# Adding two half tiles by DMA in two transfers of 64 partitions, with the adjacency copied by ScalarE, in a four-layer graph kernel

## The chip, the cores and the metric

The kernel runs on one core of a Trainium2 chip. Time is device time of one execution in microseconds (us); lower is better. The core has four compute engines, each with its own queue of instructions that it takes in order: PE (matmul), DVE (VectorE), ACT (ScalarE) and POOL (GpSimd). A fifth queue, SP, only issues transfers. Transfers are carried by 16 DMA engines that all queues share. SBUF is the working memory of 128 partitions; PSUM, in eight banks of 128 x 512 floats, takes what PE writes.

## The reference, cut to what matters

Four layers, each a residual on a normalised and rectified input. `x` is (64, 256, 128), `adj` (256, 256), all float32.

```python
h = jnp.maximum(_layernorm(x, axis=-1), 0.0); x = x + _L0_gnn_ref(h, adj, adj, ..., 5)   # gated, 5 steps
h = jnp.maximum(_layernorm(x, axis=-1), 0.0); x = x + _L1_gnn_ref(h, adj, adj, Theta1, bias)
h = jnp.maximum(_layernorm(x, axis=-1), 0.0); x = x + _L2_gnn_ref(h, adj, weight, bias)
h = jnp.maximum(_layernorm(x, axis=-1), 0.0); x = x + _L3_gnn_ref(h, adj, b_lin, a, adj)

def _L3_gnn_ref(x, W, b_lin, a, bias):
    ...
    pre = s1[:, :, None, :] + s2[:, None, :, :] + b_lin
    h = jnp.where(pre >= 0, pre, ALPHA * pre)
    e = jnp.einsum('bije,e->bij', h, a) + bias
    attn = jax.nn.softmax(e, axis=2)
    out = jax.nn.sigmoid(jnp.einsum('bij,bjf->bif', attn, x))
    return out
```

The last layer is most of the work: for each of 64 batches and each of 256 x 256 pairs of nodes, 256 features are passed through a leaky rectifier and summed with the weights `a`.

## The kernel before

**Slots and tiles.** The batches are taken in 32 pairs. The scores `e` of a pair are made in 64 slots; a slot stands for four rows `i` in each of two batches. The 256 features lie on the 128 partitions in two halves. So a slot has two tiles, half 0 and half 1, each of 128 partitions x 2048 floats (1 MB), from a ring of 14 (line 99). A tile holds, for every pair of nodes, the smaller (or the rectified difference) of a row of `s1` and all of `s2`. PE then sums over the partitions with a window of signs (`win`, `win_n`) into a bank of scores (`score`, lines 1025 to 1049, matmul on line 1041): four groups of 32 columns for a tile, which stand in the profile as eight matmul records.

**Who makes a tile.** `work_on_tile` (line 933): half 0 is made by DVE in one instruction (line 953), half 1 by ACT in eight (line 961), and POOL makes either in eight (line 967), whichever is behind.

**Added slots.** In a share of the slots, `SHARE` = 4/13 (lines 25 and 893, 600 of the 1952 slots that are not among the last 96), half 1 is made by POOL in the sign of half 0, and the two tiles are added by a DMA that POOL issues: `add_pair` (lines 985 to 993) takes the tile `z` and adds it to `t` in place (`accum_op=OP.add`, line 987). The sum is scored once, where an unjoined slot is scored twice.

**The bank of scores.** A unit is 32 slots, that is, half of the nodes `i` of a pair of batches. Its bank is filled before its first scoring, by `fill_bank` (lines 1004 to 1007): DVE writes `adj_n` (the bias of the scores) plus `lin`, a row that is the same for all `i` and comes to all partitions by a broadcast DMA (`rows`, line 783). When a unit is scored in full, `tail` (lines 827 to 882) makes softmax and output from the bank: two instructions on line 839, maximum, exponential, transpose, product, tanh, and the store. Units of the first pair (`alone`) are filled by PE instead and get their `lin` in the tail (line 834).

**Fronts.** The first three layers, and the projections that the fourth needs, are `front` (lines 498 to 821), one for each pair of batches, run beside the slots of an earlier pair. They use all four engines.

**The order.** It is fixed when the kernel is built. A planner (lines 1096 to 1137) keeps a clock for each engine, takes the engine that is earliest, and gives it what is ready by its own estimates: `ran(engine, us, ...)` adds an estimated duration. The estimates are constants: `PROJECT`, `TURN` and others on lines 471 to 473, and `ISSUE, ADDED, LANDED = 0.65, 5.3, 6.6` on line 29 for an added pair (POOL's issue, the spacing of two additions, the time from issue to landing). The order of each engine is then kept as program order; where an estimate is too short, an engine waits at run time with all behind it.

Of the kernel before, what the change touches and what calls it, by code (L numbers as in the profile page):

```python
# [10 lines left out]
OP = mybir.AluOpType  # L11
# [3 lines left out]
P = 128  # L15
NB = 2
# [5 lines left out]
MOST_POSITIVE = -MOST_NEGATIVE  # L22
PE, DVE, ACT, POOL = ENGINES = (mybir.EngineType.PE, mybir.EngineType.DVE, mybir.EngineType.Activation, mybir.EngineType.Pool)
SLOTS = 64
SHARE = (4, 13)
AHEAD_OF = 2
ALONE = 96
LOW = 1
# [4 lines left out]
def kernel(  # L33
# [50 lines left out]
    nc = tc.nc  # L84
    B, N, D = x.shape
# [20 lines left out]
    def ran(engine, us, *after):  # L106
        start = max(clock[engine], 0.0, *after)
        clock[engine] = start + us
        return clock[engine] + SEEN[engine]
# [10 lines left out]
    def of_spare(bank):  # L120

        return [b for b in spare if bank < 2 or id(b[0]) in WRITTEN]
# [14 lines left out]
    def by_feature(b, nb=NB):  # L137
        return b[:, 0:nb * N].rearrange("p (b n) -> p b n", b=nb)
# [329 lines left out]
    SHORT = dict(tag="short", bufs=12)  # L468


    PROJECT, MIX, TURN, PRODUCT, PRODUCTS = (None, 0.44, 0.86), (None, 0.88, 1.74), (None, 0.38, 0.60), (None, 0.45, 0.88), (None, 1.33, 2.64)
    COPY, BIASED, TANH, ELEMENTS = (None, 0.32, 0.48), (None, 0.40, 0.58), (None, 0.40, 0.57), (None, 0.36, 0.61)
    NORMED, STATS, LAST = (None, 0.78, 1.55), (None, 0.50, 0.87), (None, 0.55, 1.04)

    def norm(src, since, h):

        nb = src.shape[1]
        stats = work.tile([P, nb * NC, 3], F32, name="stats", bufs=4)
        mv = work.tile([P, nb * NC, 2], F32, name="mv", bufs=4)
        s, h = rows_of(src), rows_of(h)[:, :, 0:D]  # L480
        yield DVE, since
        for k in range(0, nb * NC, 2):
            nc.vector.bn_stats(stats[:, k:k + 2, :].rearrange("p k s -> p (k s)"), s[:, k:k + 2, :].rearrange("p k d -> p d k"))
        nc.vector.tensor_reduce(mv[:, :, 0], stats[:, :, 1:2], AX.X, OP.add, negate=True)
        t = ran(DVE, STATS[nb], since) + 0.1
        yield POOL, t
        inverse_root(mv[:, :, 1], stats[:, :, 2], 1.0 / D, OP.mult, LN_EPS, OP.add)
        nc.gpsimd.tensor_mul(mv[:, :, 0], mv[:, :, 0], mv[:, :, 1])  # L488
        t = ran(POOL, 1.69, t)
        yield ACT, t  # L490
        for k in range(nb * NC):
            nc.scalar.activation(h[:, k, :], s[:, k, :], AF.Relu, bias=mv[:, k, 0:1], scale=mv[:, k, 1:2])  # L492
        return ran(ACT, NORMED[nb], t)

    READY = {}
# [331 lines left out]
    def tail(u, pe, since):  # L827

        ops = READY[u]
        x3, h3, pe = ops["x3"], ops["h3"], [by_feature(pe[0])[:, k, :] for k in range(NB)]  # L830
        yield DVE, max(since, ops["t_lin"])
        used = banks_of.pop(u)[0]
        if ops["alone"]:
            nc.vector.tensor_add(by_feature(used), by_feature(used), ops["lin"].to_broadcast([P, NB, N]))
            since = ran(DVE, ELEMENTS[2], since, ops["t_lin"])
            yield DVE, since
        sc = feat("sc", **SHORT)
        for k, (b, c) in enumerate(across(u)):
            nc.vector.scalar_tensor_tensor(sc[:, k, :], ops["s2o"][:, b, :], ops["s1o"][:, b, c:c + 1], pe[k], op0=OP.min, op1=OP.add)
        t = ran(DVE, 0.8, since)  # L840
        spare.append([used, t])
        yield DVE, t
        nmx = work.tile([P, NB], F32, name="nmx")
        nc.vector.tensor_reduce(nmx, sc, AX.X, OP.max, negate=True)
        t = ran(DVE, ELEMENTS[2], t)
        yield ACT, t
        for b in range(NB):
            nc.scalar.activation(sc[:, b, :], sc[:, b, :], AF.Exp, bias=nmx[:, b:b + 1], scale=1.0)
        t_s = ran(ACT, 0.8, t)
        yield PE, t_s, 1  # L850
        b = take()
        to_token(b[0], sc)
        t = ran(PE, TURN[2], t_s, b[1])
        yield ACT, t
        wT = tok("wT", **SHORT)
        nc.scalar.copy(wT, by_token(b[0]))
        t = ran(ACT, COPY[2], t)
        spare.append([b[0], t])
        yield PE, t, 1
        bank = take()  # L860
        po = bank[0][:, :NB * (D + 1)].rearrange("p (b d) -> p b d", b=NB)
        for k, (b, _) in enumerate(across(u)):
            for c in range(NC):
                side_by_side(po[:, k, :], wT[:, k, c, :], h3[:, b, c, :], c == 0, c == NC - 1)
        t = ran(PE, PRODUCT[2], t, bank[1])
        yield DVE, t
        rs = work.tile([P, NB], F32, name="rs")
        nc.vector.reciprocal(rs, po[:, :, D])
        t = t_s = ran(DVE, 0.15, t)
        yield ACT, t  # L870
        for k in range(NB):
            nc.scalar.activation(po[:, k, 0:D], po[:, k, 0:D], AF.Tanh, scale=rs[:, k:k + 1])
        t = ran(ACT, 0.9, t, t_s)
        yield DVE, t
        o = work.tile([P, NB, D], F32, name="o")
        nc.vector.scalar_tensor_tensor(o, po[:, :, 0:D], 0.5, x3[:, 0] if ops["alone"] else x3[:, :, u[1], :], op0=OP.mult, op1=OP.add)
        t = ran(DVE, 0.36, t)
        spare.append([bank[0], t])
        p, k = u
        nc.sync.dma_start(out[p * NB + k].rearrange("(c p) d -> p c d", p=P) if ops["alone"] else  # L880
                          out[p * NB:(p + 1) * NB, k * P:(k + 1) * P, :].rearrange("b p d -> p b d"), o)
        TAILED.add(u)
# [101 lines left out]

    def add_pair(n):
        (since, t, e), (since_z, z, e_z) = pairs[n][0], pairs.pop(n)[2]
        nc.gpsimd.dma_start(out=t.rearrange("p g b n -> p (g b n)"), in_=z.rearrange("p g b n -> p (g b n)"), accum_op=OP.add)  # L987
        issued = ran(POOL, ISSUE, since, since_z)
        done = adding[0] = max(adding[0] + ADDED, issued + LANDED)
        held[e] -= 1  # L990
        held[e_z] -= 1
        tiles.append([z, done])
        made.append((done, n, 2, t, None))
# [3 lines left out]
    def bank_ready():  # L997

        u = next((u for u in UNITS if u not in left and u not in banks_of), None)
        if u not in READY or READY[u]["alone"] or len(banks_of) == 2 or all(where(slot(k))[0] < u for k in range(3)):  # L1000
            return None
        return (max(READY[u]["t_lin"], min(b[1] for b in of_spare(2))), u) if of_spare(2) else None

    def fill_bank(u):
        bank, free = take(2)
        nc.vector.tensor_add(by_feature(bank), adj_n[:, u[1]:u[1] + 1, :].to_broadcast([P, NB, N]), READY[u]["lin"])  # L1006
        banks_of[u] = bank, ran(DVE, ELEMENTS[2], free, READY[u]["t_lin"])

    def score_ready():

# [85 lines left out]
    while scored[0] < 2 * NSLOT or CHAINS:  # L1096
        while begun_fronts[0] < NPAIR and begun_fronts[0] < 2 + (scored[0] + 2 * SLOTS - 1) // (2 * SLOTS):
            begin_front()
        e = min(now, key=now.get)
        todo = []  # L1100
        for key in CHAINS:
            since = chain_ready(key, e)
            if since is not None:
                todo.append((since, (0, key) if isinstance(key, tuple) else (1, key), key))
        if e == PE:
            best = score_ready()
            if best:
                todo.append((best[0], (2,), best[1]))
        else:
            since = tile_ready(e)  # L1110
            if since is not None:
                todo.append((since, (3,), None))
            if e == DVE and bank_ready():
                todo.append((bank_ready()[0], (2,), bank_ready()[1]))
            pair = pair_ready()
            if e == POOL and pair and e not in begun:
                todo.append((pair[0] + SLACK, (2,), pair[1]))
        ready = [x for x in todo if x[0] <= now[e] + 0.05]
        if ready:
            if e == PE and len(tiles) <= LOW:  # L1120
                ready = [x for x in ready if x[1] == (2,)] or ready
            _, (rank, *_), what = min(ready, key=lambda x: x[1])
            if rank < 2:
                advance(what)
            elif e == PE:
                score(what)
            elif e == DVE and rank == 2:
                fill_bank(what)
            elif rank == 2:
                add_pair(what)  # L1130
            else:
                work_on_tile(e)
            in_order()
            now[e] = max(now[e], clock[e])
        else:
            later = [x[0] for x in todo] + [t for t in now.values() if t > now[e]]
            now[e] = min(later) if later else now[e] + 1.0
# [31 lines left out]
```

## Time and profile before

| | us |
|---|---|
| median of 2 runs | 4814.04 (4812.59 to 4815.49) |
| the profiled execution | 4794.9 |
| its span, first to last instruction | 4793.1 |

The granted clock of PE was 0.997 over the span. The lines below are for orientation; those that the argument needs are shown with it. A line of the costliest groups names the source line, engine and operation, output and inputs, shapes and count; behind the bar stand the busy time in us, the mean duration of one in ns, and the idle time just before them with what ended it. Durations of one include its start-up, so that instructions in a row overlap and the busy time is less than count times mean.

```profile
L1041 PE MATMUL bank<-rl,win_n 128*32 128x512 f32 x17864 | 2226.3, 594 | 19.9 <-DMA rl<-rl 13.4
L1041 PE MATMUL bank<-rl,win 128*32 128x512 f32 x10104 | 1349.9, 594 | 0.0
L987 POOL DMA_DIRECT2D rl<-rl x600 | 651.7, 1105 | 9.4 <-issue 4.8
rl<-rl POOLq DMA_DIRECT2D x600, 1024.0 KB, 8.1
```

The first two are the scorings, 27968 records for 3496 of them. The third are the 600 additions as POOL issues them; the fourth, from the list of DMA issues, has their size and the median time from issue to landing.

### The profile page before, as it was taken

To read this page: it belongs to the slowest core of one execution; us is meant where nothing else is said; L and a number is where in the kernel's file an instruction comes from. 1 tells how busy PE (TensorE), PEld (TensorE's weight loads), DVE (VectorE), ACT (ScalarE), POOL (GpSimd) and SP (SyncE) were. 2 spreads that over 40 slices of the span, in tenths; PEclk is the share of its full clock that TensorE was granted. 3 is DMA by queue.
4 is the path that set the end of the run, shared out by engine and by line. 5 is a ranking of instruction groups with operands and counts; after the bars stand their busy time and mean duration, and the time that the engine had idled before them with its cause. 6 is when DMAs were issued, how large, how long until landed. Compare 5 with 4: busy or idle time off the path is not lost.

```text
span 4793.1 us, 132928 instructions
## 1 busy us (share of the span) xinstructions
PE 4718.4 (98%) x51591; PEld 1740.7 (36%) x51591; DVE 4647.5 (97%) x3502; ACT 4659.3 (97%) x12220; POOL 4619.2 (96%) x9823
## 2 busy tenths in 40 slices
PE   9999999999999999999999999999999999999999
PEld 4333333333333333333333333333333333333333
DVE  5999999999999999999999999999999999999998
ACT  5999999999999999999999999999999999999999
POOL 2999999999999999999999999999999999999998
PEclk9999999999999999999999999999999999999999
DMA  0777777777777777777777777777767776777730
GB/s 23 157 143 152 146 152 150 144 149 154 152 143 154 146 146 157 147 151 145 150 146 155 149 148 147 149 151 154 148 139 153 155 150 142 145 151 148 147 69 5
DMA packets 131523, 672.70 MB, mean 140 GB/s; under 512 B 14920, under 2 KB 50120, under 8 KB 54088
## 3 DMA queue, kind: packets, MB, share of 16 engines
q0 software_dynamic: 86400, 629.18, 65.5%
q1 hardware_dynamic: 43768, 35.01, 2.5%
q8 instruction: 403, 6.60, 0.5%
q14 instruction: 232, 1.90, 0.1%
q10 hardware_dynamic: 720, 0.00, 0.0%
HBM read 26.48 MB, written 8.52 MB: 7 GB/s over the span
## 4 chain that ended last, share of the span: by engine, by line
PE 47%; DVE 15%; POOL 11%; ACT 8%; DMA 4%; issue 4%; POOLq 0%; DVEq 0%; ACTq 0%
PE bank L1041 31%; PE bank L414 14%; DVE rl L953 11%; POOL rl L967 9%; ACT rl L961 6%; DMA rl<-rl 4%; PE bank L447 1%; POOL rl L987 1%; DVE bank L1006 1%; ACT h L492 1%; PE bank L439 0%; DVE bank L626 0%; POOL mv L409 0%; DVE hT L630 0%; DVE d L622 0%
## 5 line engine op out<-in xcount | busy, mean ns | idle before, releaser
L961 ACT ACTIVATE rl<-bank,s1b 128x256 f32<-128x256 f32 x10104 | 4072.5, 833 | 10.1 <-DMA rl<-rl 6.5
L953 DVE TENSOR_TENSOR rl<-s1a,bank 128x2048 f32<-128x2048 f32 x1743 | 3894.9, 2277 | 26.1 <-DMA rl<-rl 13.1
L967 POOL TENSOR_SCALAR rl<-s2n,s1b 128x256 f32<-128x256 f32 x6280 | 3033.4, 829 | 13.9 <-DMA rl<-rl 3.1
L1041 PE MATMUL bank<-rl,win_n 128*32 128x512 f32 x17864 | 2226.3, 594 | 19.9 <-DMA rl<-rl 13.4
L1041 PE MATMUL bank<-rl,win 128*32 128x512 f32 x10104 | 1349.9, 594 | 0.0
L967 POOL TENSOR_SCALAR rl<-s2c,s1a 128x256 f32<-128x256 f32 x2440 | 1190.6, 783 | 5.2 <-PE bank L1041 1.4
L1041 PEld LDWEIGHTS bank<-rl,win_n 128*32 128x32 f32 x17864 | 583.5, 110 | 1181.0 <-issue 964.9
L987 POOL DMA_DIRECT2D rl<-rl x600 | 651.7, 1105 | 9.4 <-issue 4.8
L1041 PEld LDWEIGHTS bank<-rl,win 128*32 128x32 f32 x10104 | 335.1, 110 | 675.6 <-issue 529.4
L414 PE MATMUL bank<-mT,wts 128*32 128x512 f32 x2480 | 325.6, 595 | 4.5 <-DVE rh L587 4.5
L414 PE MATMUL bank<-adj_t,h 128*32 128x256 f32 x4960 | 297.8, 380 | 5.1 <-ACT h L641 5.0
L414 PEld LDWEIGHTS bank<-adj_t,h 128*32 128x32 f32 x4960 | 157.7, 110 | 165.8 <-ACT h L641 40.8
L492 ACT ACTIVATE h<-x,mv 128x128 f32<-128x128 f32 x376 | 170.4, 654 | 22.7 <-POOL mv L488 22.4
L583 ACT ACTIVATE bank<-bank,gate_b 128x512 f32<-128x512 f32 (+1 forms) x165 | 158.3, 959 | 17.1 <-PE bank L414 15.3
L414 PE MATMUL bank<-mT,w 128*32 128x512 f32 x1240 | 163.2, 596 | 0.0
L414 PE MATMUL bank<-rh,u5t 128*32 128x512 f32 x1240 | 162.7, 595 | 0.0
L414 PE MATMUL bank<-hT,wts 128*32 128x512 f32 x1240 | 162.1, 593 | 0.0
L539 ACT COPY mT<-bank 128x512 f32<-128x512 f32 x155 | 145.3, 937 | 16.0 <-PE bank L414 15.9
L606 ACT ACTIVATE bank<-bank,gate_b 128x512 f32<-128x512 f32 (+1 forms) x165 | 153.7, 931 | 6.1 <-PE bank L414 5.8
L619 ACT ACTIVATE bank<-bank,gate_b 128x512 f32<-128x512 f32 x155 | 147.2, 950 | 5.3 <-PE bank L414 5.2
L414 PEld LDWEIGHTS bank<-mT,wts 128*32 128x32 f32 x2480 | 81.0, 110 | 191.8 <-issue 132.5
L409 POOL TENSOR_TENSOR mv<-mv,minus_half 128x4 f32<-128x4 f32 (+1 forms) x132 | 134.2, 1017 | 11.0
(207 smaller groups left out, 3252.7 us busy)
## 6 DMA issues: line engine op xcount, KB each, us to landing
rl<-rl POOLq DMA_DIRECT2D x600, 1024.0 KB, 8.1
rows<-row SPq DMA_DIRECT2D x31, 512.0 KB
xin<-in_x_dram SPq DMA_DIRECT2D x64, 128.0 KB
out_dram<-o SPq DMA_DIRECT2D x64, 128.0 KB
row<-quarter SPq DMA_DIRECT2D x62, 2.0 KB
rows<-row SPq DMA_DIRECT2D x2, 256.0 KB
w_raw<-in_L_gnn_w_w_dram SPq DMA_DIRECT2D x3, 128.0 KB
rl<-in_L_gnn_Theta_dram SPq DMA_DIRECT2D x1, 320.0 KB
```

Of the source, the lines that this page charges most:

```text
L409: nc.gpsimd.tensor_tensor(t, t, minus_half[:, 0:t.shape[1]], op=OP.pow)
L414: nc.tensor.matmul(o[g:g + 32], w[:, g:g + 32], t, start=start, stop=stop, skip_group_check=True)
L492: nc.scalar.activation(h[:, k, :], s[:, k, :], AF.Relu, bias=mv[:, k, 0:1], scale=mv[:, k, 1:2])
L539: nc.scalar.copy(c, seen(bank))
L583: nc.scalar.activation(seen(r), seen(pr), AF.Tanh, bias=br, scale=0.5)
L606: nc.scalar.activation(seen(pr), seen(pr), AF.Tanh, bias=bz, scale=0.5)
L619: nc.scalar.activation(seen(pv), seen(pv), AF.Tanh, bias=bh_n, scale=-1.0)
L953: nc.vector.tensor_tensor(t, rows.to_broadcast(whole), ops["s2a"].unsqueeze(1).to_broadcast(whole), op=OP.min)
L961: nc.scalar.activation(t[:, g, b, :], other(ops["s2b"], b), AF.Relu, bias=rows[:, g, b], scale=-1.0)
L967: nc.gpsimd.tensor_scalar(t[:, part, b, :], other(ops["s2n" if k else "s2c"], b), rows[:, part, b], MOST_NEGATIVE, op0=OP.min, op1=OP.max)
L987: nc.gpsimd.dma_start(out=t.rearrange("p g b n -> p (g b n)"), in_=z.rearrange("p g b n -> p (g b n)"), accum_op=OP.add)
L1041: nc.tensor.matmul(pe[g * 32:(g + 1) * 32, :], w[:, 31 - r:63 - r], flat(t[:, g]), start=False, stop=(left[u] == 0), skip_group_check=True)
```

## The change

Four things change.

1. `SHARE` goes from 4/13 to 1/3: 650 of the 1952 slots are added.
2. `add_pair` issues two DMAs, one for partitions 0 to 63 and one for 64 to 127, each of 512 KB, one after the other from POOL's queue. The estimates for an added pair stay.
3. `fill_bank` is ACT's: it copies `adj_n` to the bank. `lin` is added in `tail` by DVE, for every unit, as it was for those of the first pair; the filling no longer waits for `t_lin`.
4. Two estimates of the planner grow by 0.1 (`TURN`, a transpose) and 0.4 (the statistics of `norm`).

```diff
-SHARE = (4, 13)
+SHARE = (1, 3)
...
-    ... TURN ... = ... (None, 0.38, 0.60) ...
+    ... TURN ... = ... (None, 0.48, 0.70) ...
...
-        t = ran(DVE, STATS[nb], since) + 0.1
+        t = ran(DVE, STATS[nb], since) + 0.5
...
-        used = banks_of.pop(u)[0]
-        if ops["alone"]:
-            nc.vector.tensor_add(by_feature(used), by_feature(used), ops["lin"].to_broadcast([P, NB, N]))
-            since = ran(DVE, ELEMENTS[2], since, ops["t_lin"])
-            yield DVE, since
+        used, lin = banks_of.pop(u)[0], ops["lin"]
+        nc.vector.tensor_add(by_feature(used), by_feature(used), lin.to_broadcast([P, NB, N]) if ops["alone"] else lin)
+        since = ran(DVE, ELEMENTS[2], since, ops["t_lin"])
+        yield DVE, since
...
-        nc.gpsimd.dma_start(out=t.rearrange("p g b n -> p (g b n)"), in_=z.rearrange("p g b n -> p (g b n)"), accum_op=OP.add)
+        for h in range(0, P, P // 2):
+            nc.gpsimd.dma_start(out=t[h:h + P // 2].rearrange("p g b n -> p (g b n)"),
+                                in_=z[h:h + P // 2].rearrange("p g b n -> p (g b n)"), accum_op=OP.add)
...
-        return (max(READY[u]["t_lin"], min(b[1] for b in of_spare(2))), u) if of_spare(2) else None
+        return (min(b[1] for b in of_spare(2)), u) if of_spare(2) else None
...
-        nc.vector.tensor_add(by_feature(bank), adj_n[:, u[1]:u[1] + 1, :].to_broadcast([P, NB, N]), READY[u]["lin"])
-        banks_of[u] = bank, ran(DVE, ELEMENTS[2], free, READY[u]["t_lin"])
+        nc.scalar.copy(by_feature(bank), adj_n[:, u[1]:u[1] + 1, :].to_broadcast([P, NB, N]))
+        banks_of[u] = bank, ran(ACT, 0.51, free)
...
-            if e == DVE and bank_ready():
+            if e == ACT and bank_ready():
...
-            elif e == DVE and rank == 2:
+            elif e == ACT and rank == 2:
```

## The prediction

> **What bounds the kernel now.** I read the page's busy shares and DMA queues first, then the chain that ended last, then the costliest groups, and after that the stages, single lines and the timeline where the change bites.
>
> ```profile
> PE 4718.4 (98%) x51591; PEld 1740.7 (36%) x51591; DVE 4647.5 (97%) x3502; ACT 4659.3 (97%) x12220; POOL 4619.2 (96%) x9823
> ...
> q0 software_dynamic: 86400, 629.18, 65.5%
> q1 hardware_dynamic: 43768, 35.01, 2.5%
> ...
> PE 47%; DVE 15%; POOL 11%; ACT 8%; DMA 4%; issue 4%; POOLq 0%; DVEq 0%; ACTq 0%
> ```
>
> Four compute engines are full together; the DMA engines, filled almost wholly by the additions of two half tiles (queue q0), have a third of their time free. The chain passes from engine to engine, and only 4% of it stands on a landing addition. The stages say the same: in the row of one whole millisecond (busy time of each engine, granted clock, DMA share, GB/s) four engines stand near 985 of 1000 us and DMA at 0.73.
>
> ```profile
> 1000.00:2000.00 1000.00, 987.39 (x10884) 358.84 (x10880) 985.76 (x730) 984.73 (x2582) 986.91 (x2096) 1.00 0.73 150
> ```
>
> So DMA is the one resource with slack, and 27% is the whole of it. The additions at their one line (minimum/median/maximum ns, first and last start; below it the time from issue to landing), and the page's groups of the tiles that feed them:
>
> ```profile
> L987 POOL DMA_DIRECT2D rl<-rl x600: 591/990/2751, 117.7 to 4592.2; - x150
> ...
> DMA to landing us min/median/max: 6.7/8.1/15.2
> ```
> ```profile
> L961 ACT ACTIVATE rl<-bank,s1b 128x256 f32<-128x256 f32 x10104 | 4072.5, 833 | 10.1 <-DMA rl<-rl 6.5
> L953 DVE TENSOR_TENSOR rl<-s1a,bank 128x2048 f32<-128x2048 f32 x1743 | 3894.9, 2277 | 26.1 <-DMA rl<-rl 13.1
> L967 POOL TENSOR_SCALAR rl<-s2n,s1b 128x256 f32<-128x256 f32 x6280 | 3033.4, 829 | 13.9 <-DMA rl<-rl 3.1
> ...
> L967 POOL TENSOR_SCALAR rl<-s2c,s1a 128x256 f32<-128x256 f32 x2440 | 1190.6, 783 | 5.2 <-PE bank L1041 1.4
> ```
>
> A tile costs 3894.9/1743 = 2.23 us on DVE, 4072.5/(10104/8) = 3.22 on ACT, (3033.4+1190.6)/(8720/8) = 3.88 on POOL. Together they make 0.448+0.310+0.258 = 1.016 tiles per us, so one microsecond more of work on DVE, ACT or POOL costs 0.44, 0.31 or 0.25 us of span once the plan has spread it.
>
> **The additions in halves.** This term decides. Now: 86400 packets/600 = 144 for one addition, 128 rows of 8 KB and 16 more, one for each of 16 engines; each engine takes 8 rows. Their time is 0.655 x 16 x 4793.1/600 = 83.7 us of engine time, 5.23 us on each of 16, 0.654 us for a row. With the change an engine has 4 rows of the first half and 4 of the second, in the same queue: the same eight rows. By the row alone an addition still takes 5.23 us, 650 of them 3,400 us, 71% of the span, and nothing waits.
>
> The Trainium skill speaks against this: "SBUF — State Buffer", section "Door 1: The DMA port swizzle", says that SBUF is reached by DMA through 16 ports, that partitions 0 to 63 have only eight of them and 64 to 127 the other eight, at about 27.2 GB/s a port; its section on issuing two DMAs for the two halves gives only 6% over a single one. No transfer of 64 wide partitions is in this trace, so it neither agrees nor disagrees. What the trace does show is that a port has no room for two: the sum reads both tiles, 16 KB in 0.654 us, 25 GB/s per engine. If two engines share one port, a row takes between 16 KB x 2 / 27.2 GB/s = 1.20 us (estimate from that page's rate) and twice today's, 1.31. An addition is then 8 such rows, 9.6 to 10.5 us, since the second half stands behind the first on every engine. I take 10.0, nearer the measured row's double less the gaps that a neighbour can fill. The sums by the two: 3,400 us of DMA against 650 x 10.0 = 6,500, more than the span. I side with the rule, because it names the shape that the diff makes and the rate agrees with how full one engine's reads are.
>
> Then DMA is the bound, and the sum is: 118 us before the first addition (its row's first start); 6,500; 140 for the other queues, whose 3.1% of 4793 is 149 us on the same engines; the gaps in which no addition is queued; and 4793 - 4592 = 201 us after the last issue, where the plan has no additions. Gaps lie between 0 and 8.1 - 5.2 = 2.9 us each (every addition issued only after the one before had landed). The plan issues one every (4592 - 118)/600 = 7.5 us on average, sooner than 10.0, and the 14 tiles let it run ahead, so I take 0.3: 195 us. Total 7,154 us of span. The profiled execution lasted 4794.9 beside a span of 4793.1 and a median of 4814.04, 0.4% more, so the time is about 7,180.
>
> Who waits: POOL issues in order, and PE scores in an order fixed when the kernel is built. A sum that is planned to land after 6.6 us lands after 12 or more; PE stands at its first matmul on it (line 1041) with all projections and transposes of the fronts queued behind; then no tile comes free and DVE, ACT and POOL stop at their next one.
>
> **The share, 4/13 to 1/3.** Of 1952 slots 650 are added in place of 600. Each saves PE one scoring. In the timeline of PE eight records follow eight at 0.86 us:
>
> ```profile
> 2004.05 1.04 PE L1041 MATMUL bank<-rl,win 128*32 128x512 f32 x8
> 2004.90 1.04 PE L1041 MATMUL bank<-rl,win_n 128*32 128x512 f32 x8
> 2005.76 1.04 PE L1041 MATMUL bank<-rl,win 128*32 128x512 f32 x8
> ```
>
> So PE loses 50 x 0.86 = 43 us, worth at most that if PE alone bound. At 10.0 us an addition the same 50 cost 500 us of DMA, which is in the sum.
>
> **POOL's issues.** The mean of 1105 ns overlaps the operations behind it; the timeline shows what an issue really takes:
>
> ```profile
> 2000.88 1.16 POOL L987 DMA_DIRECT2D rl<-rl  x1
> 2001.51 4.11 POOL L967 TENSOR_SCALAR rl<-s2n,s1b 128x256 f32<-128x256 f32 x8
> ...
> 2016.87 1.91 POOL L987 DMA_DIRECT2D rl<-rl  x2
> 2018.04 11.27 POOL L967 TENSOR_SCALAR rl<-s2n,s1b 128x256 f32<-128x256 f32 x24
> ```
>
> 0.63 us from one issue to the next operation, 1.17 for two. Now 600 x 0.63 = 378 us. Half a transfer has half the rows: it costs from 0.29 (all of it goes by rows) to 0.59 (none). 1300 of them are 377 to 767 us; I take 0.45, 585, which is 207 more and 207 x 0.25 = 53 us of span if POOL binds. Behind a DMA bound it costs nothing; that cover is gone if the halves run at full rate.
>
> **The adjacency's copy.**
>
> ```profile
> L1006 DVE TENSOR_TENSOR bank<-adj_n,rows x62: 677/847/5343, 238.1 to 4662.6; 128x512 f32<-128x512 f32 x62
> ```
> ```profile
> L834 DVE TENSOR_TENSOR bank<-bank,rows x2: 691/692/692, 191.2 to 263.3; 128x512 f32<-128x512 f32 x2
> ```
>
> 62 adds of two SBUF operands took 85.7 us in all (mean 1382 ns); the form that takes their place, bank plus rows, took 692 ns. DVE saves 62 x 0.69 = 43 us. ACT gets 62 copies; a 128x512 copy started at 2010.00 there and the next operation at 2010.48, so 62 x 0.47 = 29 us. In span: -19 and +9. The filling no longer waits for the broadcast rows; the add in the tail does, with the scores of that unit and DVE's next tiles behind it, but rows have long landed by then (line 834 waited 0). The unit's chain is 0.69 us longer, covered by tiles everywhere but in the last unit: +0.7 us.
>
> **The plan's numbers.** 0.1 us more for a transpose and 0.4 for statistics move instructions, not work. Bounds are +/-20 us, what POOL idled outside the first microseconds before such results; I take 0.
>
> **Rivals.** (1) The halves run at full rate: the ports are not what limits an accumulating row, or two engines drift so that one reads the low half while the other reads the high. Then DMA stays at 71%, the compute engines bind as now, and the elementwise sum is -19 + 9 + 53 = +43, at best -19 + 9 + 0 = -10, at worst +92; PE is 43 us lighter. That is 4,785 to 4,890 of span, likeliest 4,835, about 4,850 as a median: not slower by 2%. The place is line 987's packets, and the point is exact: compute needs 4793 - 118 - 201 - 149 = 4,325 us for 650 additions, 6.65 each, 0.83 us a row. Below 0.83 this rival holds; above it DMA binds. For it speaks that every row of the trace is a whole transfer at 0.654; against it, that one engine's reads alone come to 25 GB/s. (2) Ports are shared but partly overlapped, rows of 0.85 to 1.15 us: 650 x 6.8 to 9.2 plus 460 gives 4,900 to 6,450, near 5,500. (3) The second half is taken for a write of the same tile and POOL waits for the first to land: at least 6.7 us of waiting each (the minimum to landing), 650 x 8 or more with POOL stopped, 7,500 and up. Against it: pairs of loads of `xin` into parts of one tile show no wait of that kind. It ends on the same side as the forecast and is held inside its upper end.
>
> **How the numbers follow.** Full sharing 0.80 (the third rival in it): 6,560 (9.6 us, no gaps) to 7,900 (10.5 us and 1 us of gap: 650 x 11.5 + 460 = 7,935). Partial sharing 0.06. Full rate 0.14: most of it within 2%, a few hundredths slower by dear issues or faster by the lighter PE. A measurement here tells about 2% from no change. Range 5,300 to 7,900: it leaves out the full rate and the far ends, together about 0.2. Slower 0.86, within 2% 0.11, faster 0.03; time 7,180.
>
> **What would show it.** Right: q0's share near 90% with about 104,000 packets (650 x 160), a row's time of 1.2 to 1.3 us (q0's share x 16 x span / 650 / 128), landings of 12 us or more, PE idle before line 1041 by hundreds of us on landing additions, all engines near 65%. Wrong: q0 near 71%, landings still about 8 us, engines still at 96% or more. Line 1006 on ACT should be near 0.8 us a copy, and the add in the tail 0.69.

## The result, and the profile after

The changed kernel takes 5572.65 us (median of 2 runs, 5563.24 to 5582.07) against 4814.04: 1.1575 of before, interval 1.1556 to 1.1594. It is slower by 16%, where the forecast had half as much again. The profiled execution was the one of 5582.07 us.

From the page of the changed kernel: busy time of each engine, the two main DMA queues (packets, MB, share of 16 engines), the chain that ended last by engine and by line.

```profile
PE 4907.6 (88%) x51191; PEld 1868.1 (33%) x51191; DVE 4651.7 (83%) x3509; ACT 4732.2 (85%) x12266; POOL 5160.2 (92%) x10483
...
q0 software_dynamic: 104000, 681.66, 86.2%
q1 hardware_dynamic: 43768, 35.01, 2.1%
...
DMA 40%; PE 22%; POOL 20%; DVE 8%; ACT 6%; issue 4%; POOLq 0%; DVEq 0%; ACTq 0%
DMA rl<-rl 40%; POOL rl L966 15%; PE bank L1042 13%; PE bank L414 8%; DVE rl L952 6%; ACT rl L960 4%; POOL rl L987 4%; PE bank L447 1%; POOL mv L409 1%; PE bank L439 0%; DVE stats L483 0%; ACT h L492 0%; DVE bank L626 0%; DVE d L622 0%; DVE hT L630 0%
```

The DMA engines have gone from 65.5% to 86.2% for additions, and landings from 4% of the chain to 40%. But PE, DVE and ACT lost only 10 to 14 points of their share, not the 30 or so of the forecast, and POOL is busier than any of them. One whole millisecond (columns as before: busy time of PE, PE's weight loads, DVE, ACT and POOL, granted clock, DMA share, GB/s), then the additions at their line, with what waited for them:

```profile
1000.00:2000.00 1000.00, 869.12 (x9065) 324.18 (x9069) 831.10 (x609) 843.50 (x2183) 935.17 (x1892) 0.95 0.94 136
```
```profile
L987 POOL DMA_DIRECT2D rl<-rl x1300: 568/1149/3781, 111.8 to 5369.7; - x186
...
who waited for it (us, times):
  PE bank L1042: 562.8, 275
  DVE rl L952: 262.0, 122
  PEld bank L1042: 200.6, 42
  ACT rl L960: 179.3, 82
  POOL rl L966: 104.0, 61
...
DMA to landing us min/median/max: 7.1/12.2/22.1
```

In the middle DMA is taken 94% of the time; it was 73%. PE waits 562.8 us at its scoring line for landings, where it waited 13.4 before. The median landing comes 12.2 us after the issue, where the plan counts 6.6. So the bound is the forecast's. Its size is not: q0 gives 0.862 x 5580.3/650 = 7.40 us for an addition, and 16 x 7.40/128 = 0.925 us for a row. In the terms of the forecast's sum: 112 us before the first addition, 650 x 7.40 = 4,810, 145 for the other queues (2.6%) and 211 after the last issue; the gaps are what is left of the span, 302. That they are so small agrees with the 6% of the time between the first and the last issue in which the DMA engines were not taken, 315 us of 5,258.

### The profile page after: what moved, and what is told of

Read it like the earlier page. It is cut to its first block, busy times and chain, and to the rows that moved or that the text cites. A ratio compares the mean times of both kernels' runs of the same rounds, so it can differ in the third digit from the quotient of the medians.

```text
span 5580.3 us, 133831 instructions
## 1 busy us (share of the span) xinstructions
PE 4907.6 (88%) x51191; PEld 1868.1 (33%) x51191; DVE 4651.7 (83%) x3509; ACT 4732.2 (85%) x12266; POOL 5160.2 (92%) x10483
## 3 DMA queue, kind: packets, MB, share of 16 engines
q0 software_dynamic: 104000, 681.66, 86.2%
## 4 chain that ended last, share of the span: by engine, by line
DMA 40%; PE 22%; POOL 20%; DVE 8%; ACT 6%; issue 4%; POOLq 0%; DVEq 0%; ACTq 0%
DMA rl<-rl 40%; POOL rl L966 15%; PE bank L1042 13%; PE bank L414 8%; DVE rl L952 6%; ACT rl L960 4%; POOL rl L987 4%; PE bank L447 1%; POOL mv L409 1%; PE bank L439 0%; DVE stats L483 0%; ACT h L492 0%; DVE bank L626 0%; DVE d L622 0%; DVE hT L630 0%
## 5 line engine op out<-in xcount | busy, mean ns | idle before, releaser
L960 ACT ACTIVATE rl<-bank,s1b 128x256 f32<-128x256 f32 x10088 | 3932.5, 627 | 202.5 <-DMA rl<-rl 179.3
L966 POOL TENSOR_SCALAR rl<-s2n,s1b 128x256 f32<-128x256 f32 x6296 | 3198.5, 1039 | 112.3 <-DMA rl<-rl 63.0
L1042 PE MATMUL bank<-rl,win_n 128*32 128x512 f32 x17480 | 2324.7, 618 | 578.1 <-DMA rl<-rl 562.8
L1042 PE MATMUL bank<-rl,win 128*32 128x512 f32 x10088 | 1394.9, 608 | 1.3 <-issue 1.2
L987 POOL DMA_DIRECT2D rl<-rl x1300 | 1312.8, 1336 | 56.5 <-issue 22.5
L1042 PEld LDWEIGHTS bank<-rl,win 128*32 128x32 f32 x10088 | 372.0, 112 | 674.0 <-issue 517.4
L539 ACT COPY mT<-bank 128x512 f32<-128x512 f32 x155 | 104.4, 673 | 124.8 <-PE bank L414 124.4
L587 DVE SCALAR_TENSOR_TENSOR rh<-bank,hT 128x512 f32<-128x512 f32 x155 | 106.4, 687 | 112.3 <-ACT bank L583 112.0
L583 ACT ACTIVATE bank<-bank,gate_b 128x512 f32<-128x512 f32 (+1 forms) x165 | 118.7, 719 | 85.9 <-PE bank L414 53.2
L641 ACT COPY h<-bank 128x512 f32<-128x512 f32 x124 | 85.3, 688 | 86.5 <-PE bank L447 85.6
L606 ACT ACTIVATE bank<-bank,gate_b 128x512 f32<-128x512 f32 (+1 forms) x165 | 125.1, 758 | 28.9 <-PE bank L414 28.6
## 6 DMA issues: line engine op xcount, KB each, us to landing
rl<-rl POOLq DMA_DIRECT2D x1300, 512.0 KB, 12.2
```

What stands on the lines that cost most here:

```text
L539: nc.scalar.copy(c, seen(bank))
L583: nc.scalar.activation(seen(r), seen(pr), AF.Tanh, bias=br, scale=0.5)
L587: nc.vector.scalar_tensor_tensor(rh, seen(r), 1.0, hT, op0=OP.add, op1=OP.mult)
L606: nc.scalar.activation(seen(pr), seen(pr), AF.Tanh, bias=bz, scale=0.5)
L641: nc.scalar.copy(h, turned_of(b))
L960: nc.scalar.activation(t[:, g, b, :], other(ops["s2b"], b), AF.Relu, bias=rows[:, g, b], scale=-1.0)
```

## The experiments

The question was why a row took 0.925 us, neither the 0.65 of whole transfers nor the 1.3 of two engines on one port, and whether DMA was all of it. "Row" below is always q0's share x 16 x span / rows added, a row being the 8 KB of one partition.

**The split undone.** `e1_whole` is the changed kernel with line 987 as before.

> The changed kernel with each addition issued again as one transfer of 128 partitions; the share of 1/3, the copy on ACT, the add in the tail and the plan's numbers stay. Shared ports: the row goes back to 0.65 us, DMA to 650 x 5.2 = 3,400 us (about 71%), the compute engines bind again, about 4,790 us (4,750 to 4,850). If the share or the copy had a part in the loss, it stays above 4,900.

```diff
-        for h in range(0, P, P // 2):
-            nc.gpsimd.dma_start(out=t[h:h + P // 2]..., in_=z[h:h + P // 2]..., accum_op=OP.add)
+        nc.gpsimd.dma_start(out=t..., in_=z..., accum_op=OP.add)
```

(`...` stands for the rearranging of `t` and `z`.) 4801.24 us, 0.9979 of before (0.9970 to 0.9988). Its page:

```profile
PE 4684.8 (98%) x51191; PEld 1735.4 (36%) x51191; DVE 4621.8 (97%) x3509; ACT 4681.9 (98%) x12266; POOL 4622.0 (97%) x9833
...
q0 software_dynamic: 93600, 681.62, 71.1%
```

The row is 0.654 again with all 650 additions. The whole loss goes with the split.

**The split alone**, on the kernel before.

> The kernel before with the split alone (600 additions of two halves). Shared ports with the row of 0.92 us that the changed kernel showed: 600 x 7.4 = 4,440 us of DMA, and with 118 before, 145 of other queues, about 290 of gaps and 200 after, 5,190 us. If POOL's issues pace the kernel: 700 fewer DMAs to issue than half... no, 600 more issues of 0.57 us on POOL, 340 us x 0.25, about 4,900 us. If the other parts cause the loss: near 4,815.

5565.25 us, 1.1566 (1.1539 to 1.1593): as slow as the changed kernel, though with 600 additions, so the expectation of 5,190 fell. The row was 0.977 (q0 84.3% of 5560.5 us). An addition has no fixed price: with fewer of them each one was dearer. Two questions follow: what makes a row dear, and what else holds the kernel.

**Halves by columns, and halves in turns.** Two cuts that leave the number of transfers and bytes alone: by columns, each transfer with all partitions, and by partitions with the order turned in every other addition (`tf` and `zf` are the two tiles with each partition's elements in one row).

> The changed kernel with the two transfers cut by columns: each has all 128 partitions and 1024 of the 2048 elements of a row. As many issues, as many bytes, as many transfers. Shared ports: no two engines meet on a port, 8 KB take about 0.65 us again (two pieces of 0.33), DMA near 72%, only POOL's 650 further issues of 0.57 us remain (370 us x 0.25 = 90), about 4,880 us. If POOL's issues or the smaller transfers are the cause: 5,570 us as in the changed kernel.

> The changed kernel with the order of the halves turned in every other addition (low, high, high, low). If a long queue is quick because two engines of a port fall one half out of step, so that one reads the low half while the other reads the high, that offset now meets the same half every second time: rows of 1.0 us and more in the mean, 6,000 to 6,700 us. If a port serves two engines at the measured mean in any order, nothing changes: 5,570 us.

```diff
 e3_columns
+        for h in range(0, 8 * N, 4 * N):
+            nc.gpsimd.dma_start(out=tf[:, h:h + 4 * N], in_=zf[:, h:h + 4 * N], accum_op=OP.add)
 e4_turns
+        turn[0] = not turn[0]
+        for h in ((0, P // 2) if turn[0] else (P // 2, 0)):
+            nc.gpsimd.dma_start(out=tf[h:h + P // 2], in_=zf[h:h + P // 2], accum_op=OP.add)
```

By columns: 5370.82 us, 1.1161 (1.1137 to 1.1185). In turns: 6233.39 us, 1.2951 (1.2926 to 1.2975). First the queue's line for columns, then for turns:

```profile
q0 software_dynamic: 187200, 681.66, 67.6%
```
```profile
q0 software_dynamic: 104000, 681.66, 91.1%
```

In turns a row took 1.09 us with the same transfers, only ordered otherwise: the cost of a row depends on what stands next to it in the queue, as engines out of step would have it. By columns the row fell to 0.70, so it is the choice of partitions, not the number of transfers, that makes rows dear. Yet the time is 570 us above the whole transfers, not the 90 expected, with DMA 74% taken in the middle. The engines of this run, its chain, and its rows for POOL:

```profile
PE 5038.6 (94%) x51191; PEld 1856.3 (35%) x51191; DVE 4645.5 (87%) x3509; ACT 4716.8 (88%) x12266; POOL 5212.5 (97%) x10483
...
POOL 52%; PE 26%; ACT 7%; DMA 6%; issue 5%; DVE 3%; POOLq 0%; SPq 0%; DVEq 0%; ACTq 0%
...
L988 POOL DMA_DIRECT2D rl<-rl x1300 | 1840.7, 2148 | 0.6 <-issue 0.3
```
```profile
2036.47 1.76 POOL L988 DMA_DIRECT2D rl<-rl  x2
2037.72 4.09 POOL L966 TENSOR_SCALAR rl<-s2n,s1b 128x256 f32<-128x256 f32 x8
2041.28 2.26 POOL L988 DMA_DIRECT2D rl<-rl  x2
...
2049.62 2.72 POOL L988 DMA_DIRECT2D rl<-rl  x2
2050.79 5.13 POOL L966 TENSOR_SCALAR rl<-s2n,s1b 128x256 f32<-128x256 f32 x8
2054.35 3.29 POOL L988 DMA_DIRECT2D rl<-rl  x2
```

Half of the chain is POOL. In the timeline (start, time in us) the starts look harmless: two issues and the next operation 1.2 us on. But each pair lasts longer than the one before, 1.76, 2.26, 2.72, 3.29: something behind the starts falls back about 0.5 us with each pair, so the starts understate an issue. POOL was busy for 5212.5 us, against 4622.0 with whole transfers, and its instructions differ by the 650 further issues alone: 590 us, or 0.91 each. By the span it is 570 us, or 0.88 each.

**POOL's issues told to the plan.** Both cuts once more with `ISSUE` 1.6 on line 29 in place of 0.65; nothing else differs.

> The two transfers by columns (5,371 us) with ISSUE at 1.6. There DMA had slack and POOL stood in 52% of the chain. If the loss there is that 1300 issues take some 0.8 us each of POOL and the plan counts 0.65 for two, the plan now spreads about 600 us of POOL at 0.25 us of span for each: 4,800 + 150 = 4,950 us (4,900 to 5,020). If two transfers are slow in themselves, it stays at about 5,370.

> The changed kernel with the planner's ISSUE at 1.6 in place of 0.65, so that the plan knows what two issues cost POOL and gives POOL fewer tiles. If the shared ports alone hold the changed kernel, DMA stays the bound and the time stays at 5,450 to 5,600 us with POOL's idle time up. If POOL's unplanned issues hold it, POOL is relieved of some 600 us and the time falls to 4,900 to 5,050.

By columns 4932.97 us, 1.0242 (1.0227 to 1.0257), as expected: 438 us of the 570 were POOL work that the plan did not know and so did not move. The changed kernel with the same number: 5453.39 us, 1.1330 (1.1311 to 1.1349), 119 us less, at the lower edge of what was expected if the ports alone hold it, and far from the 4,900 to 5,050 of the other case. Its queue and PE's scoring:

```profile
q0 software_dynamic: 104000, 681.66, 86.9%
```
```profile
L1042 PE MATMUL bank<-rl,win_n 128*32 128x512 f32 x17016 | 2249.9, 611 | 527.6 <-DMA rl<-rl 503.2 <-DVE rl L952 16.1 <-POOL rl L966 6.9
```

PE still waits 503.2 us for landings. DMA is the bound of the changed kernel, and POOL's issues are a second one close behind it: by columns, where DMA had room, they alone took the kernel to 5,371 us.

**The port by itself.** One transfer of 64 partitions for an addition: partitions 0 to 63, or 32 to 95. The other partitions are not added, so the times stand for no working kernel; the rows can be compared.

> One transfer for each addition, of partitions 0 to 63 alone; partitions 64 to 127 of the tiles are not added. As many issues as with whole transfers, half the bytes. All transfers use the same eight ports, so no step out of line helps: if two engines share a port, every row takes 1.25 to 1.35 us and a transfer of four rows an engine lasts about 5.2 us, from issue to landing about 7 us. If ports are not shared: rows of 0.65 us, landing after about 4.3 us. The time stays near 4,800 either way, since DMA has slack.

> The same as the run with the low partitions, for partitions 32 to 95; the others are not added. Also 64 partitions and 512 KB, but they lie half on the low ports and half on the high, one engine for each port. Shared ports: rows of 0.65 us, landing after about 4.3 us. If it is the number of partitions that slows a transfer, rows as in the run with the low ones.

```diff
+            nc.gpsimd.dma_start(out=tf[0:64], in_=zf[0:64], accum_op=OP.add)       # e12_low
+            nc.gpsimd.dma_start(out=tf[32:96], in_=zf[32:96], accum_op=OP.add)     # e13_middle
```

4758.41 and 4756.14 us in one run each. The queue and the time to landing, low first:

```profile
q0 software_dynamic: 52000, 340.83, 70.9%
```
```profile
DMA to landing us min/median/max: 7.0/7.9/14.8
```

and in the middle:

```profile
q0 software_dynamic: 52000, 340.83, 36.3%
```
```profile
DMA to landing us min/median/max: 4.1/4.8/8.0
```

The same packets and bytes take twice the engine time when they lie on partitions 0 to 63: rows of 1.30 us against 0.66. This is the sharing that the forecast took from the port map, at the upper of its two ends (1.31). Whether it is the reading of the two tiles or the writing of the sum that meets at a port, no run tells.

**Out of step or not.** With a share of 1/12 nearly every addition starts on idle engines.

> The changed kernel with a share of 1/12, 162 additions of two halves in place of 650, so that nearly every addition starts on idle DMA engines. If the mean row of 0.92 us comes of engines that have fallen out of step in a long queue, they start in step here and share nearly every row: a mean of 1.15 to 1.3 us and a second half that lands about 12 us after its issue. If 0.92 belongs to each addition by itself, the mean stays at 0.92. The time rises by PE's 488 further scorings of 0.86 us, to about 5,200 us, and says nothing here.

```profile
q0 software_dynamic: 25920, 169.89, 29.5%
```

The row is 0.295 x 16 x 5566.4/(162 x 128) = 1.27 us. So two halves into an empty queue share almost every row; in the full queue of the changed kernel the mean is 0.925. The trace's packets of the changed kernel show the two kinds: 47% of the rows took 0.60 to 0.66 us, 30% took 1.2 us or more, 18% lay between 0.72 and 1.2. Where the quick rows lie can be seen in the sparse run, whose additions stand apart in the trace. Of the rows of the first half 0.4% took under 0.72 us, of the first 16 of the second half 48%, of the 48 after them 0.9%. So a row is quick where the queue changes from one half to the other. What one change saves can be estimated from the row of 1.30 us in which all is shared, 10.38 us for eight: 10.38 - 10.13 = 0.25 us in the sparse run, which has one, (10.38 - 7.40)/2 = 1.49 in the changed kernel, which has two for each addition, and 10.38 - 8.73 = 1.65 in turns, which has one. In a standing queue a change is worth six times what it is in an empty one. That the engines of one port fall further out of step there fits all of these figures, but is inferred: the packets carry no engine's name, and that the halves overlap within one engine is not ruled out.

The time, 5568.2 us in one run, is some 370 above what was expected from PE's scorings. Landings make 20% of its chain, and a half landed after 9.6 us (the median) where the plan counts 6.6; how much of the 370 that explains was not followed up.

**The other parts, and a version that beats both.** Whole transfers throughout: the share alone, the copy and the tail's add alone, and everything else of the change with `ISSUE` at 0.85.

> The kernel before with the share of 1/3 alone, whole transfers. PE is 43 us lighter, POOL has 50 issues more; by the planner's balance between nothing and 20 us faster: 0.996 to 1.0 of before. If the share made DMA or POOL worse, slower than before.

> The kernel before with the copy on ACT and the add in the tail alone, whole transfers, share 4/13, the plan's old numbers. DVE saves 43 us at 0.44, ACT gains 29 at 0.31: 10 us faster, 0.998 of before (0.995 to 1.0).

> Whole transfers, everything else as changed, with the planner's ISSUE at 0.85 in place of 0.65, near what a further issue cost POOL in the run with columns (570 us for 650). If the plan gains from knowing it, 4,770 to 4,795 us, below both kernels; if the overlap behind an issue hides the rest, as the run with whole transfers, 0.998 of before.

The share alone: 4840.27 us, 1.0066 (1.0046 to 1.0086), slower by a little. The copy alone: 4777.36 us, 0.9936 (0.9911 to 0.9962), below the 0.995 to 1.0 expected; it is the fastest of those that add all partitions, and below both kernels. Everything with the dearer issue in the plan: 4790.30 us, 0.9965 (0.9955 to 0.9975), below the kernel before but no clear gain on the 0.9979 of whole transfers with the old `ISSUE`. The copy's two lines in the changed kernel (minimum/median/maximum ns):

```profile
L1007 ACT COPY bank<-adj_n x62: 574/720/1601, 258.5 to 5446.7; 128x512 f32<-128x512 f32 x62
```
```profile
L833 DVE TENSOR_TENSOR bank<-bank,rows x64: 690/699/700, 207.1 to 5569.6; 128x512 f32<-128x512 f32 x64
```

The add from the bank never took more than 700 ns, where the add of two SBUF operands had reached 5343. The gain is 0.0064 x 4,804 = 31 us (27 by the two medians), about three times the 10 forecast. A part of the rest is that line 1006 also held up POOL. In the kernel before, POOL's instructions for a tile start 0.45 us apart; during 41 of the 56 such adds beside which this can be measured, one of these steps was over 0.7 us (median 0.91), 20 us of POOL in all. Beside the add that starts at 977.11 us, for instance, POOL's starts are 976.79, 977.24 and then 978.13. In the copy's run no add from the bank came with a step over 0.47 us. At the forecast's 0.25 that is 5 us of span (an estimate); what the remaining 10 or so are was not measured.

## Why the prediction was wrong, point by point

- **DMA becomes the bound because two engines share a port.** Right, and shown: 1.30 against 0.66 us a row in the two runs of 64 partitions, DMA 94% taken in the middle of the changed kernel, PE waiting for landings.
- **"An addition is then 8 such rows, 9.6 to 10.5 us, since the second half stands behind the first on every engine. I take 10.0."** This is the step that failed. Measured 7.40. That nearly every row is shared holds where additions come singly (1.27 in the sparse run, 8 rows are 10.1 us). In a standing queue only a part is shared: two engines out of step work on different halves (inferred). The 6% that the forecast quotes for two transfers over one lies at the empty end too: a pair of halves runs 2% faster than the low half's rate in the sparse run and 40% faster in the changed kernel (10.4 against 10.1 and 7.4 us). The forecast had named this drift, but put it with the rival in which nothing is shared and gave the partly shared case 0.06; that case, 4,900 to 6,450 and near 5,500, is what happened. The measured time lies in the stated range of 5,300 to 7,900 only because its lower end reaches into that case. It should have had more: the standing queue that the forecast itself made the bound is what makes rows cheaper, 0.925 us against 1.27 in an empty one. The term was 650 x 2.6 = 1,690 us too large.
- **POOL's issues.** Two errors. The 1300 halves were taken at 0.45 us each. POOL's busy time in the changed kernel is 5160.2 us against 4622.0 with whole transfers, for the same operations and 650 more issues: 538 us more, 0.83 for each further issue, where 1300 x 0.45 less 650 x 0.63 would be 175. And 0.25 us of span for each of POOL's was used "once the plan has spread it", though the diff leaves `ISSUE` at 0.65 for both issues, so that the plan does not spread them. By columns, where ports are not shared, the further issues cost 570 us of span. "Behind a DMA bound it costs nothing" was wrong too, since telling the plan gave back 119 us of the changed kernel.
- **The gaps** were taken at 195 us and are 302 as the rest of the sum; the head, the tail and the other queues (118, 201, 140) were 112, 211, 145.
- **The share.** 43 us for PE was forecast to help little under DMA. With whole transfers the share alone is 0.66% slower, outside the 0.996 to 1.0 expected of that run. On its page PE waits 50.7 us for landing additions at its scoring line, where it waited 13.4, and landings make 9% of the chain in place of 4%; that this is the whole of the loss is not shown. The two parts alone multiply to 1.0066 x 0.9936 = 1.0002, near the 0.9979 of both together.
- **The copy.** Direction right, size about a third of the measured. Each took what was named, 0.72 us on ACT (0.8 forecast) and 0.70 for the add (0.69); what the old add did to POOL was left out.
- **The signs of right and wrong** named ahead: 104,000 packets came; 90% for q0 was 86.2; landings of 12 us came, and PE's wait of hundreds of us; the engines at 65% did not (83 to 92), nor the row of 1.2 to 1.3.
- **Two sums** do not come out, without bearing on the outcome: 9.6 us without gaps makes 650 x 9.6 + 460 = 6,700, not 6,560, and the worst case of the first rival is -10 + (767 - 378) x 0.25 = +87, not +92.

## What to carry to other kernels

What a transfer costs on a shared port depends on the transfers around it: measure it alone and in the queue in which it will run, and place a part of 64 partitions so that it covers both halves of the port map (here 32 to 95 ran twice as fast as 0 to 63). When an edit adds work to an engine whose order is planned from constants, look whether the constant was changed: work that the plan does not know is not spread, and where that engine comes to bind it goes into the span almost one for one (590 us of POOL were 570 of span by columns). And a rule with two clean ends need not be met at either; price the middle by what the forecast bound itself will do to the queue.

## What the hardware showed that was not expected

- A POOL issue of 64 partitions occupies POOL nearly as long as one of 128: two half issues and the start of the next operation lie 1.13 us apart in the changed kernel, two whole ones lay 1.17 apart before, and POOL's busy time with 650 issues of 64 partitions was 4592.0 (low) and 4579.7 (middle) against 4622.0 with 650 of 128, less by 0.05 to 0.07 us for each. Behind the starts a lag builds up over several additions (1.76 to 3.29 us for a pair by columns). From the changed kernel:

```profile
2022.98 2.06 POOL L987 DMA_DIRECT2D rl<-rl  x2
2024.12 4.51 POOL L966 TENSOR_SCALAR rl<-s2c,s1a 128x256 f32<-128x256 f32 x8
```

- PE's granted clock was lower in the runs in which PE waited more: 0.997 before (98% busy), 0.958 in the changed kernel (88%), 0.928 with the halves in turns (82%). For the same 51191 matmuls PE was busy 4684.8 us with whole transfers, 4907.6 in the changed kernel and 5102.5 in turns. The clock is not all of that: by columns it was 5038.6 us at a clock of 0.987.
- An add of two SBUF operands on DVE and POOL's instructions hold each other up: the 62 adds of line 1006 took from 0.68 to 5.34 us, and beside 33 of 44 that took under 1.5 us POOL lost about 0.45 us. The form with one operand in the bank did neither, 0.69 to 0.70 us.
- With 50 additions fewer the split kernel was no faster (5565 against 5573 us), since rows got dearer, 0.977 against 0.925. DMA was taken 92% of the middle there and 94% in the changed kernel, so the queue ran empty more often; that this is why the rows got dearer is inferred.
